# Layer-1 FFN of a vision tower: the elementwise work of GpSimd moves to VectorE, with a new order of the pieces

## The chip, the cores and the metric

The kernel runs on one core of a Trainium2 chip. A core has five engines with a queue each, which run on their own and wait for each other by semaphores: PE (TensorE, matmuls into PSUM), DVE (VectorE), ACT (ScalarE), POOL (GpSimd) and SP (SyncE, which here issues nearly all DMA transfers). An engine takes its queue in order, so an instruction that waits holds up all that stand behind it. The metric is the device time of one execution in microseconds (us), taken as the median of several runs.

## The reference, cut to what matters

32 images of 256 tokens with 256 features pass through a tokenizer and two layers, each with an attention and an FFN block, all in float32. The change lies in the FFN of layer 1. With four heads of 64 features and four experts a head it computes, for each image:

```python
sx = jnp.einsum('bsh,ndh->bnsd', x, hl_w) + hl_b[None, :, None, :]
q, k, v = ...                                    # from sx; q for each of 4 experts
att = jax.nn.softmax(scores + causal, axis=-1)
qkv = jnp.einsum('bnest,bntd->bnesd', att, v)
gs = jax.nn.softmax(einsum(out, gate_w) + gate_b, axis=-1)
mixed = jnp.einsum('bnsed,bnse->bnsd', out.reshape(b, nh, s, ne, d), gs)
hn = layernorm(mixed + resid, ln_g, ln_b)
hx = relu(fx @ fc1_w.T + fc1_b) @ fc2_w.T + fc2_b   # fx is hn, head by head
hx = layernorm(hx + fx, fnorm_g, fnorm_b)
fg = jax.nn.softmax(fout @ fgate_w.T, axis=-1)      # fout is hx, heads joined
h = h + fout.reshape(b, s, nh, d) * fg[..., None]
```

In `setup_inputs` the gain `fnorm_g` is all ones and the bias `fnorm_b` all zeros.

## The kernel before

The activations of all images stay in SBUF, in 32 tiles `H[b]` of 128 partitions by 512 elements (two blocks `c` of 128 tokens, 256 features each). The stages before, up to about 1229 us, are the tokenizer, layer 0 and the attention of layer 1. The change leaves them alone.

The FFN of layer 1 is cut into pieces, listed in `PIECES` by number. A piece is a small function that issues a few instructions of one engine for one image `b`: `heads` (PE), `heads_out` (ACT copies and two transfers on SP), `experts`, `head_values`, six parts of `scores` (PE), their `exponentials` (ACT) and `later_keys` (POOL, a select that zeroes the keys after the query), eight `outputs` (PE) and `outputs_out` (ACT copies to `eo`), the softmax of the experts' gate (`gate_logits`, `gate_softmax`, DVE with one exponential on ACT), `mixed` and `summed` (the experts' weighted sum), a norm (`squares` on ACT, `squares_sum` on DVE, `root` on ACT, `scaled`), `turn_e`, `moved_e` and `turned_e` (a transpose of 32x32 blocks, written to DRAM and read back turned), the two small layers `first_layer` and `second_layer` with `features_moved` for their input, and at the end the heads' gate (`head_gate`) and the final norm (`last_norm`), which writes the image out.

The order in which the pieces are issued is written by hand as numbers. `ROUND` is a list of pairs (offset, piece): one pass over it issues each piece once, each for the image that lies the offset ahead, so that about eight images are in work at once. Round after round is issued until the last image has had its `heads`; the list `END` issues what is then left. A manual schedule keeps each engine's queue in this order, and semaphores are put in where data or buffers require it. So in a steady round PE, DVE, ACT, POOL and SP do exactly one image's worth of work each.

Buffers matter too. There are eight PSUM banks, handed out in turn by `bank()`: the ninth request waits until the first has been emptied. Tiles from the pool `e_1` have one buffer for each name. The tile called `esq` holds in turn the first norm's squares, the result of the block transpose (`turn_e`, L1359), and the second norm's squares.

The places that are touched: `mixed` (L1316) multiplies the experts' outputs `eo` by their gate in two halves of 1024 elements, the first on DVE, the second on POOL. `summed` (L1326) adds the halves. `head_gate` 9 (L1458) multiplies the norm's factor `fv` by the heads' gate. `last_norm` (L1460 to L1481) computes `ey * fv` and times the gain `fn_g` on DVE, bias times gate (`fadd`, L1470) and plus `H[b]` (L1474) on POOL, adds both on DVE (L1477) and stores the sum.

Of the kernel before, what the change touches and what calls it, by code (L numbers as in the profile page):

```python
# [35 lines left out]
ALU = mybir.AluOpType  # L36
# [5 lines left out]
B, N, D = 32, 256, 256  # L42
# [38 lines left out]
def vit_tower(tc, a, out):  # L81
# [38 lines left out]
    def over(ap, shape, axis):  # L120
        return ap.unsqueeze(axis).to_broadcast(shape)
# [987 lines left out]
    with (  # L1109
# [205 lines left out]

        def mixed(b, im, k):  # L1316
            x = experts_of(im, k, MIX, HD)
            (nc.vector if k == 0 else nc.gpsimd).tensor_tensor(  # L1318
                x, x, over(im.gate[:, :, 2 * k : 2 * k + 2], [P, NG, 2, HD], 3), ALU.mult
            )  # L1320

# [33 lines left out]
        def turn_e(b, im):  # L1355
            if b == B - 1:
                im.pt = feature_major(im.whole["er"].rearrange("p (c n) d -> p c (n d)", c=NC))
                return
            y = whole(im, "esq", G8, key="blocks").rearrange("p g d -> p (g d)")  # L1359
            nc.vector.transpose(  # L1360
                y.rearrange("p (f s t) -> p s f t", f=4, t=32),
                im.whole["er"].rearrange("p (c k m) d -> p k c (m d)", c=2, k=2),
            )
            im.d = dram.tile([2, 4, 32, N], F32, name="er_turned", bufs=4)
            nc.sync.dma_start(im.d.rearrange("m i q x -> (i q) m x"), y.rearrange("p (m x) -> p m x", m=2))
# [65 lines left out]
        def head_gate(b, im, i):  # L1431
# [22 lines left out]
                nc.vector.reciprocal(im.m, im.m)  # L1454
            if i == 8:
                nc.vector.tensor_tensor(im.gate, im.gate, over(im.m, [P, NC, NH], 2), ALU.mult)
            if i == 9:
                nc.vector.tensor_tensor(im.rs, im.rs, im.gate.rearrange("p c n -> p (c n)"), ALU.mult)  # L1458

        def last_norm(b, im, i):  # L1460
            if i == 0:
                f = whole(im, "fout", G8)
                nc.vector.tensor_tensor(f, im.whole["ey"][:, :, 0:HD], over(im.rs, G8, 2), ALU.mult)  # L1463
            if i == 1:
                f = im.whole["fout"]
                nc.vector.tensor_tensor(f, f, over(row_e("fn_g"), G8, 1), ALU.mult)  # L1466
            if i == 2:
                w = whole(im, "fadd", G8)
                nc.gpsimd.tensor_tensor(
                    w, over(row_e("fn_b"), G8, 1), over(im.gate.rearrange("p c n -> p (c n)"), G8, 2), ALU.mult  # L1470
                )
            if i == 3:
                w = im.whole["fadd"]
                nc.gpsimd.tensor_tensor(w, w, H[b].rearrange("p c (n d) -> p (c n) d", d=HD), ALU.add)  # L1474
            if i == 4:
                f = im.whole["fout"]
                nc.vector.tensor_tensor(f, f, im.whole["fadd"], ALU.add)  # L1477
                nc.sync.dma_start(
                    out[b].rearrange("(c p) d -> p c d", p=P),
                    f.rearrange("p (c n) d -> p c (n d)", n=NH),  # L1480
                )  # L1481

        images = [Image() for _ in range(B)]
        PIECES = (
            (features_in,), (residual,), (moved_e,), (heads,), (heads_out,), (experts, 0), (experts_out, 0),
# [10 lines left out]
            (squares_sum, 0), (root, 0), (scaled,), (turn_e,), (turned_e,), (features_zero,), (first_layer,),  # L1496
            (first_layer_out,), (second_layer,), (second_layer_out, 0), (second_layer_out, 1), (squares, 1),
            (squares_sum, 1), (root, 1), (head_gate, 0), (head_gate, 1), (head_gate, 2), (head_gate, 3),
            (head_gate, 4), (head_gate, 5), (head_gate, 6), (head_gate, 7), (head_gate, 8), (head_gate, 9),
            (last_norm, 0), (last_norm, 1), (last_norm, 2), (last_norm, 3), (last_norm, 4),  # L1500
            (features_moved,),
        )
        ROUND = (
            (-11, 9), (-12, 6), (-10, 54), (-7, 85), (-10, 55), (-7, 86), (-10, 56), (-7, 87), (-10, 57),
            (-11, 30), (-13, 3), (-10, 58), (-11, 10), (-8, 69), (-11, 17), (-7, 89), (-8, 70), (-13, 4),
            (-13, 1), (-11, 25), (-11, 23), (-12, 12), (-11, 11), (-12, 16), (-7, 88), (-12, 22), (-10, 59),
            (-7, 90), (-11, 29), (-8, 68), (-13, 7), (-9, 2), (-12, 18), (-11, 36), (-10, 60), (-11, 27),
            (-10, 61), (-11, 33), (-11, 44), (-8, 71), (-11, 32), (-10, 62), (-13, 8), (-11, 31), (-11, 40),
            (-8, 72), (-11, 41), (-10, 63), (-8, 73), (-7, 91), (-8, 74), (-10, 64), (-12, 24), (-8, 75),
            (-11, 39), (-11, 34), (-8, 76), (-11, 38), (-11, 35), (-8, 77), (-11, 42), (-8, 78), (-11, 43),  # L1510
            (-11, 37), (-12, 14), (-11, 46), (-11, 45), (-10, 65), (-11, 47), (-8, 79), (-12, 28), (-12, 15),
            (-11, 48), (-8, 80), (-8, 81), (-11, 49), (-9, 67), (-12, 20), (-11, 50), (-12, 26), (-13, 5),
            (-8, 82), (-12, 13), (-11, 51), (-9, 92), (-11, 52), (-10, 66), (-8, 83), (-15, 0), (-11, 53),
            (-12, 21), (-8, 84), (-12, 19),
        )
        END = (
            (2, 10), (3, 58), (4, 2), (2, 25), (2, 27), (2, 11), (5, 69), (3, 59), (6, 88), (5, 70), (2, 17),
            (1, 16), (1, 9), (3, 60), (0, 4), (1, 10), (2, 31), (3, 61), (2, 23), (5, 68), (2, 36), (2, 39),
            (2, 33), (1, 22), (3, 62), (3, 63), (4, 67), (5, 71), (2, 35), (2, 29), (2, 38), (5, 72),
            (5, 73), (1, 11), (4, 92), (2, 34), (3, 64), (3, 65), (2, 37), (5, 74), (5, 75), (6, 89),  # L1520
            (2, 44), (2, 41), (1, 28), (2, 32), (2, 42), (6, 90), (1, 17), (2, 43), (3, 66), (5, 76), (0, 2),
            (6, 91), (2, 46), (2, 40), (5, 77), (5, 78), (5, 79), (2, 45), (2, 47), (2, 48), (5, 80),
            (1, 23), (2, 49), (1, 29), (0, 7), (5, 81), (2, 50), (1, 14), (2, 51), (2, 52), (2, 53), (5, 82),
            (4, 69), (2, 54), (2, 55), (0, 5), (0, 8), (1, 15), (5, 83), (4, 70), (1, 20), (2, 56), (1, 13),
            (5, 84), (2, 57), (2, 58), (0, 6), (0, 12), (1, 12), (1, 21), (1, 19), (0, 16), (0, 18), (1, 18),
            (3, 2), (4, 71), (4, 68), (2, 59), (1, 38), (1, 27), (2, 60), (4, 72), (2, 61), (1, 25), (1, 36),
            (1, 37), (4, 73), (1, 24), (0, 22), (1, 32), (2, 62), (1, 26), (1, 35), (0, 24), (3, 67),
            (5, 85), (2, 63), (5, 89), (1, 46), (4, 74), (1, 45), (2, 64), (5, 86), (1, 44), (5, 90),
            (1, 33), (5, 87), (4, 75), (4, 76), (3, 92), (5, 88), (2, 65), (2, 66), (1, 31), (1, 39),
            (1, 34), (1, 40), (1, 43), (1, 41), (1, 42), (1, 47), (1, 48), (1, 49), (0, 14), (4, 77),  # L1530
            (1, 50), (4, 78), (1, 51), (4, 79), (0, 20), (3, 69), (1, 52), (1, 53), (3, 70), (1, 54),
            (0, 15), (1, 55), (0, 13), (0, 9), (0, 26), (0, 17), (0, 21), (4, 80), (1, 56), (1, 57), (4, 81),
            (0, 10), (2, 2), (3, 68), (0, 11), (4, 82), (1, 58), (4, 83), (0, 23), (4, 84), (0, 31), (4, 85),
            (0, 19), (1, 59), (3, 71), (0, 25), (0, 27), (3, 72), (1, 60), (0, 30), (0, 33), (2, 67),
            (1, 61), (0, 32), (3, 73), (0, 34), (0, 28), (0, 39), (1, 62), (0, 35), (0, 43), (0, 29),
            (2, 68), (0, 36), (1, 63), (0, 40), (5, 91), (0, 42), (1, 64), (3, 74), (2, 92), (1, 65),
            (0, 44), (4, 89), (0, 37), (0, 38), (3, 75), (4, 86), (0, 41), (0, 46), (0, 45), (1, 66),
            (0, 47), (3, 76), (0, 48), (3, 77), (0, 49), (3, 78), (0, 50), (2, 69), (3, 79), (2, 70),
            (0, 51), (0, 52), (4, 87), (0, 53), (0, 54), (0, 55), (1, 2), (2, 71), (3, 80), (4, 90), (0, 56),
            (3, 81), (0, 57), (3, 82), (0, 58), (1, 67), (4, 88), (1, 69), (1, 92), (2, 72), (3, 83),  # L1540
            (0, 59), (3, 84), (0, 60), (3, 85), (0, 61), (4, 91), (0, 62), (2, 73), (1, 70), (0, 63),
            (2, 74), (0, 64), (1, 68), (2, 75), (2, 76), (0, 65), (2, 77), (3, 86), (2, 78), (2, 79),
            (3, 89), (3, 87), (2, 80), (0, 66), (2, 81), (1, 71), (2, 82), (3, 90), (0, 67), (3, 88),
            (2, 83), (1, 72), (2, 84), (3, 91), (2, 85), (1, 73), (0, 92), (1, 74), (1, 75), (1, 30),
            (1, 76), (1, 77), (2, 89), (2, 86), (0, 69), (1, 78), (2, 87), (1, 79), (1, 80), (2, 90),
            (1, 81), (2, 88), (0, 70), (1, 82), (1, 83), (0, 71), (1, 84), (2, 91), (1, 85), (0, 72),
            (1, 89), (0, 73), (1, 86), (0, 74), (0, 75), (1, 87), (0, 76), (0, 77), (0, 78), (0, 79),
            (1, 90), (0, 80), (0, 81), (1, 88), (0, 82), (0, 83), (0, 84), (1, 91), (0, 85), (0, 89),
            (0, 68), (0, 86), (0, 87), (0, 90), (0, 88), (0, 91),
        )  # L1550
        LATE = {1: B // 2 - 2, 2: B // 2 - 1}
        LAST = PIECES.index((heads,))

        def order_e():
# [422 lines left out]
```

## Time and profile before

| what | value |
|---|---|
| median of 3 runs | 1882.4 us (1880.36 to 1883.76) |
| the profiled execution's own time | 1881.05 us |
| its span, first to last instruction | 1879.3 us |
| mean granted TensorE clock | 0.99 |
| start of the layer-1 FFN (first load of `exT`) | 1228.9 us |
| distance of rounds from 1343 us to 1790 us | 18.62 us |
| last `heads`, where `END` begins | 1790.5 us |

The profile shows one execution. Busy times of an engine are the union of its instructions; the ends of matmuls are modelled, so PE seems busier than it is. In a windows row the columns are the stretch, its length, then for PE, PEld (weight loads), DVE, ACT and POOL the busy time with the number of instructions, then the granted clock, the DMA share and GB/s. In a timeline row they are start, duration, engine, line, operation, output<-inputs, the shapes and the number of instructions merged. In a waits row: who waited, for whom, total us, times, longest. A wait for several semaphores is put down to the one that came last.

### The profile page before, as it was taken

The numbers are of one execution on the slowest core, as the hardware profiler recorded it, in microseconds if no ns is written. First come the engines' busy times: TensorE is split into PE (matmuls) and PEld (weight loads), VectorE is DVE, ScalarE is ACT, GpSimd is POOL, SyncE is SP. The second block draws the span as 40 slices with busy tenths as digits, with TensorE's granted clock in tenths as the row PEclk, the third lists the DMA queues.
The fourth block names the chain that finished last, engine by engine and source line by source line (L and its number), as shares of the span: only waits on it lengthen the run. The fifth ranks groups of instructions, "written<-read, shape, count | busy, mean of one in ns | idle before, by whom it ended". The sixth has DMA issues, their size and how long they took to land. (4 is left out here: it accounts for less than half of the span.)

```text
span 1879.3 us, 36625 instructions
## 1 busy us (share of the span) xinstructions
PE 1829.4 (97%) x14282; PEld 1286.5 (68%) x14282; DVE 1346.5 (72%) x3336; ACT 800.0 (43%) x1640; POOL 827.1 (44%) x792
## 2 busy tenths in 40 slices
PE   9999999999999999999999999999999999999993
PEld 7887567676767676766655555567877777787872
DVE  2335376878787674534578778746899989998998
ACT  0001222222222212121344554557878787877772
POOL 1224133434343334243353433424575757676653
PEclk9999999999999999999999999999999999999995
DMA  8540221212121134233222222122343333333332
GB/s 302 162 153 19 46 56 45 68 45 64 38 63 39 68 120 138 85 118 93 87 79 79 79 79 79 68 79 61 92 106 98 103 103 98 103 98 103 97 86 69
DMA packets 193171, 167.50 MB, mean 89 GB/s; under 512 B 70880, under 2 KB 166112, under 8 KB 192608
## 3 DMA queue, kind: packets, MB, share of 16 engines
q1 hardware_dynamic: 186272, 147.51, 27.3%
q0 software_dynamic: 6144, 16.79, 2.9%
q8 instruction: 115, 1.88, 0.4%
q10 hardware_dynamic: 576, 0.79, 0.1%
q14 instruction: 64, 0.52, 0.1%
HBM read 82.98 MB, written 57.41 MB: 75 GB/s over the span
## 5 line engine op out<-in xcount | busy, mean ns | idle before, releaser
L1237 POOL TENSOR_SCALAR_AFFINE_SELECT et<-et 128x1024 f32<-128x1024 f32 (+1 forms) x192 | 199.4, 1059 | 206.5 <-ACT et L1228 185.7
L118 PE MATMUL bank<-ev,et 128*64 128x72 f32 (+1 forms) x6144 | 204.2, 225 | 3.9 <-DVE ev L1203 2.3
L118 PEld LDWEIGHTS bank<-ev,et 128*64 128x64 f32 x6144 | 193.3, 137 | 17.7 <-POOL fadd L1474 7.6
L1228 ACT ACTIVATE et<-bank 128x512 f32<-128x512 f32 x384 | 199.6, 624 | 3.1 <-PE bank L118 1.7
L118 PE MATMUL bank<-g,sx 64*128 64x512 f32 (+1 forms) x512 | 194.4, 501 | 0.3 <-ACT g L1190 0.3
L118 PE MATMUL bank<-g,sw 64*128 64x512 f32 (+1 forms) x512 | 189.9, 501 | 0.9 <-DVE ev L1203 0.9
L118 PE MATMUL bank<-tokW,patch 128*128 128x256 f32 x768 | 166.6, 379 | 3.1 <-DMA patch<-in_patches_dram 3.1
L118 PEld LDWEIGHTS bank<-tokW,patch 128*128 128x128 f32 x768 | 145.9, 190 | 24.1 <-issue 3.9
L118 PE MATMUL bank<-bxT,w_wuv 128*128 128x512 f32 x300 | 131.4, 592 | 2.5 <-DMA bxT<-b_turned 2.5
L864 ACT ACTIVATE hT<-bank,cols 128x512 f32<-128x512 f32 x64 | 43.6, 687 | 187.3 <-PE bank L118 120.2
L118 PE MATMUL bank<-wvo,dm 128*128 128x512 f32 x256 | 114.3, 599 | 0.0
L118 PE MATMUL bank<-w_wo,gT 128*128 128x256 f32 x512 | 113.2, 379 | 0.0
L118 PE MATMUL bank<-attn,bv 128*128 128x256 f32 x512 | 113.1, 379 | 0.0
L118 PE MATMUL bank<-w_w,hT 128*128 128x256 f32 x512 | 112.3, 379 | 0.0
L118 PE MATMUL bank<-xsel,w_w 128*128 128x512 f32 x256 | 111.4, 592 | 0.0
L118 PEld LDWEIGHTS bank<-attn,bv 128*128 128x128 f32 x512 | 97.2, 190 | 19.6 <-issue 7.2
L118 PEld LDWEIGHTS bank<-g,sx 64*128 64x128 f32 x512 | 88.1, 186 | 31.4 <-issue 21.8
L126 DVE BATCH_NORM_STATS2 six<-h 128x6 f32<-128x256 f32 x256 | 105.6, 412 | 4.4
L118 PEld LDWEIGHTS bank<-w_w,hT 128*128 128x128 f32 x512 | 97.0, 190 | 15.6 <-issue 2.9
L118 PEld LDWEIGHTS bank<-w_wo,gT 128*128 128x128 f32 x512 | 97.2, 190 | 13.4 <-DVE gT L489 0.2
L151 POOL TENSOR_SCALAR rs_c<-st_c 128x4 f32<-128x4 f32 x16 | 3.0, 190 | 234.4 <-DVE st_c L127 234.4
L118 PE MATMUL bank<-w_wuv,bxT 128*128 128x512 f32 x240 | 105.4, 592 | 0.0
(289 smaller groups left out, 3814.6 us busy)
## 6 DMA issues: line engine op xcount, KB each, us to landing
patch<-in_patches_dram SPq DMA_DIRECT2D x31, 768.0 KB
exT<-normed SPq DMA_DIRECT2D x32, 256.0 KB
sw<-sx SPq DMA_DIRECT2D x64, 128.0 KB
out_dram<-fout SPq DMA_DIRECT2D x32, 256.0 KB
er_turned<-esq SPq DMA_DIRECT2D x31, 256.0 KB
fraw<-er_turned SPq DMA_DIRECT2D x62, 128.0 KB
both<-fxT SPq DMA_DIRECT2D x62, 128.0 KB
both<-hx SPq DMA_DIRECT2D x62, 128.0 KB
```

Source lines behind the costliest of these rows:

```text
L118: nc.tensor.matmul(o, lhsT, rhs, start=first, stop=last)
L126: nc.vector.bn_stats(six, x)
L151: nc.gpsimd.tensor_scalar(o, var, 1.0, 1e-5, ALU.mult, ALU.add)
L864: nc.scalar.activation(s.hT[:, m, :], p, AF.Gelu_apprx_tanh, bias=col("b1", m))
L1228: nc.scalar.activation(t2[:, i, :], p, AF.Exp)
L1237: nc.gpsimd.affine_select(out=own, in_=own, pattern=[[0, 2 * n_e], [1, P]], compare_op=ALU.is_ge, fill=0.0, base=0, channel_multiplier=-1,)
```

## The change

- `mixed` runs both halves on DVE.
- `last_norm` runs wholly on DVE. It is now: `ey * fv` (part 0), times `fn_g` (part 1), plus `fn_b` (part 2), and then for each of the eight groups of 64 features (two token blocks, four heads) one `scalar_tensor_tensor`, which multiplies by the heads' gate, a scalar for each token, and adds `H[b]` (parts 3 and 4). Part 5 is the store. `head_gate` 9 and the tile `fadd` are gone. In the new lists part 2 stands ahead of part 1.
- POOL is left with the six selects of `later_keys` in each round.
- The block transpose of `turn_e` writes to a tile of its own, `eblk`.
- `ROUND` and `END` are new. On PE a round now begins with `experts` 0 and three parts of `scores`, has `experts` 1, `head_values`, `first_layer`, `heads` and the other three parts of `scores` next, and ends with `second_layer` and the eight `outputs`. On DVE the two halves of the mix stand next to each other with `scaled` between, `turn_e` comes after them and ahead of the second norm's squares, and the eight operations of the final norm follow the last product of `head_gate`. `LATE` is only moved in the text.

```diff
         def mixed(b, im, k):
             x = experts_of(im, k, MIX, HD)
-            (nc.vector if k == 0 else nc.gpsimd).tensor_tensor(
+            nc.vector.tensor_tensor(
                 x, x, over(im.gate[:, :, 2 * k : 2 * k + 2], [P, NG, 2, HD], 3), ALU.mult
             )
...
-            y = whole(im, "esq", G8, key="blocks").rearrange("p g d -> p (g d)")
+            y = whole(im, "eblk", G8).rearrange("p g d -> p (g d)")
...
-            if i == 9:
-                nc.vector.tensor_tensor(im.rs, im.rs, im.gate.rearrange("p c n -> p (c n)"), ALU.mult)
 
         def last_norm(b, im, i):
+            f = whole(im, "fout", G8)
             if i == 0:
-                f = whole(im, "fout", G8)
                 nc.vector.tensor_tensor(f, im.whole["ey"][:, :, 0:HD], over(im.rs, G8, 2), ALU.mult)
             if i == 1:
-                f = im.whole["fout"]
                 nc.vector.tensor_tensor(f, f, over(row_e("fn_g"), G8, 1), ALU.mult)
             if i == 2:
-                w = whole(im, "fadd", G8)
-                nc.gpsimd.tensor_tensor(
-                    w, over(row_e("fn_b"), G8, 1), over(im.gate.rearrange("p c n -> p (c n)"), G8, 2), ALU.mult
-                )
-            if i == 3:
-                w = im.whole["fadd"]
-                nc.gpsimd.tensor_tensor(w, w, H[b].rearrange("p c (n d) -> p (c n) d", d=HD), ALU.add)
-            if i == 4:
-                f = im.whole["fout"]
-                nc.vector.tensor_tensor(f, f, im.whole["fadd"], ALU.add)
+                nc.vector.tensor_tensor(f, f, over(row_e("fn_b"), G8, 1), ALU.add)
+            if i in (3, 4):
+                for n in range(NH):
+                    g, d = (i - 3) * NH + n, slice(n * HD, (n + 1) * HD)
+                    nc.vector.scalar_tensor_tensor(
+                        f[:, g, :], f[:, g, :], im.gate[:, i - 3, n : n + 1], H[b][:, i - 3, d], ALU.mult, ALU.add
+                    )
+            if i == 5:
                 nc.sync.dma_start(
...
         PIECES = (
...
-            (head_gate, 4), (head_gate, 5), (head_gate, 6), (head_gate, 7), (head_gate, 8), (head_gate, 9),
-            (last_norm, 0), (last_norm, 1), (last_norm, 2), (last_norm, 3), (last_norm, 4),
+            (head_gate, 4), (head_gate, 5), (head_gate, 6), (head_gate, 7), (head_gate, 8), (last_norm, 4),
+            (last_norm, 0), (last_norm, 1), (last_norm, 2), (last_norm, 3), (last_norm, 5),
...
         ROUND = (
-            (-11, 9), (-12, 6), (-10, 54), (-7, 85), (-10, 55), (-7, 86), (-10, 56), (-7, 87), (-10, 57),
...
+            (-1, 84), (-4, 43), (-5, 27), (-4, 46), (-6, 5), (-5, 13), (-4, 44), (-6, 6), (-1, 85), (-1, 86),
+            (-1, 90), (-5, 19), (-5, 25), (-5, 12), (-5, 28), (-2, 2), (-2, 67), (-4, 47), (-4, 48),
...
+            (-5, 40), (-5, 38), (-2, 80), (-5, 35), (-2, 81), (-2, 88), (-2, 82), (-5, 36), (-2, 83),
```

## The prediction

> **What bounds the kernel now.** I read the page's busy table first, then the span by windows, then the waits of a steady stretch, and last the timelines of single rounds.
>
> ```profile
> PE 1829.4 (97%) x14282; PEld 1286.5 (68%) x14282; DVE 1346.5 (72%) x3336; ACT 800.0 (43%) x1640; POOL 827.1 (44%) x792
> ```
>
> PE at 97% looks like the answer, but the ends of matmuls are modelled. The windows view (length, then busy time of PE, PEld, DVE, ACT, POOL) of four rounds of the layer-1 FFN says more. The cuts are where PE starts the `heads` matmuls of one image and of the next.
>
> ```profile
> 1307.50:1325.40 17.90, 17.90 (x301) 14.21 (x299) 12.46 (x38) 15.10 (x37) 7.49 (x8) 1.00 0.36 91
> 1325.40:1343.30 17.90, 17.90 (x301) 14.38 (x299) 16.20 (x38) 14.21 (x36) 11.78 (x9) 1.00 0.36 90
> 1343.30:1361.90 18.60, 18.58 (x300) 14.73 (x298) 16.90 (x40) 14.57 (x37) 12.33 (x9) 1.00 0.38 100
> 1641.50:1660.10 18.60, 18.58 (x300) 14.76 (x298) 16.90 (x41) 14.57 (x37) 12.32 (x9) 1.00 0.39 100
> ```
>
> PE does the same work in all four. While the pipeline of images fills, DVE has 12.46 us of work and the round takes 17.9. From the third on DVE has 16.90 and the round takes 18.62, unchanged until 1790 us. So 17.87 (starts 1307.5, 1325.4, 1343.3) is what PE needs, and the 0.75 above it comes from the loop through DVE. The waits of PE over 18 steady rounds (total, times, longest) agree:
>
> ```profile
> PEld bank L118 <- DVE ev L1203: 12.0, 18, 0.7
> PEld bank L118 <- ACT g L1190: 2.9, 17, 0.2
> ```
>
> One pair of score matmuls in each round waits for the PSUM bank that DVE empties at L1203; in the round at 1641 its second half starts 0.40 late (1646.15, 1646.55). A second wait of about 0.2 stands behind ACT's copy of `g`.
>
> Why DVE is slow is in the timelines of DVE and POOL (start, duration; in brackets the idle time before and who ended it):
>
> ```profile
> 1306.87 1.22 DVE L1318 TENSOR_TENSOR eo<-eo,gate 128x1024 f32<-128x1024 f32 x1
> 1642.15 2.94 DVE L1318 TENSOR_TENSOR eo<-eo,gate 128x1024 f32<-128x1024 f32 x1
> 1647.04 2.29 DVE L1326 TENSOR_TENSOR two<-eo 128x1024 f32<-128x1024 f32 x1
> 1649.86 0.97 DVE L1329 TENSOR_TENSOR er<-two 128x512 f32<-128x512 f32 x1
> ```
>
> ```profile
> 1641.72 2.29 POOL L1318 TENSOR_TENSOR eo<-eo,gate 128x1024 f32<-128x1024 f32 x1 [0.43 <-DVE gate L1314]
> 1643.97 2.02 POOL L1469 TENSOR_TENSOR fadd<-rows_e,fgate 128x512 f32<-128x512 f32 x1
> 1646.55 1.70 POOL L1474 TENSOR_TENSOR fadd<-fadd,h 128x512 f32<-128x512 f32 x1
> 1648.21 4.74 POOL L1237 TENSOR_SCALAR_AFFINE_SELECT et<-et 128x1024 f32<-128x1024 f32 x4
> ```
>
> The two engines take turns. POOL's half of the mix ends at 1644.01, and DVE's, begun at 1642.15, ends 1.08 later. POOL's `fadd` ends at 1648.25, and `two` ends 1.08 later. Begun ahead of POOL (1306.87), DVE's mix takes 1.22. So a DVE operation with two SBUF inputs that meets a running POOL operation waits for its end, then runs at its own speed.
>
> [...] The zero counts at L1172, with one tensor input, take 0.67 beside POOL work too. [...]
>
> **The change part by part, per round.** Costs on DVE are start-to-start distances in the round at 1641.
>
> - Half of the mix moves from POOL to DVE: one more 1024-element product, 1.22 long, 1.13 to its successor. POOL's 2.29 goes, and DVE's own half no longer waits: 2.86 becomes 1.13. Net on DVE 1.13 - 1.73 = -0.60.
> - The two `fadd` operations leave POOL (2.02 + 1.70). `two` no longer waits behind the second: 2.22 becomes 1.13, -1.09.
> - The final norm: the last addition (L1477, 0.60 apart) and the small product L1458 (0.11) go; an addition of the bias comes, as L1466, 0.63. Eight `scalar_tensor_tensor` of 64 elements come. No row has that form. [...] Below: independent 48-element products L1287 start 0.11 apart, 0.9 for eight. They don't wait for each other, so I take 0.13 each, 1.05. Net +0.97.
> - Sum: 16.90 - 0.60 - 1.09 + 0.97 = 16.2 busy on DVE. Of this about 0.7 is the wait of L1329 and L1332 behind selects (0.97 and 1.00 against 0.68), which the new order may keep or move.
> - POOL keeps six selects: 12.3 - 2.29 - 2.02 - 1.70 = 6.3, less for those that now don't wait (0.63 and 1.09 free, against means of 0.86 and 1.59).
> - DVE behind selects: bounded by none, and by all of them standing in front of a two-input operation, 4 x 0.5 + 2 x 1.0 = 4. Laying the new order beside PE's pieces, selects 4, 0, 5 and 3 fall under `junk`, the transpose, PSUM evictions or a reduction, and selects 1 and 2 hold up one operation each. I take 1.0 in all, i.e. 0.3 above the old 0.7: 16.5.
> - Waits of DVE for ACT: 14.3 + 9.1 over 18 rounds, 1.3 a round. The one for `fv` (0.6) stays, since `root` and the first gate product still follow each other; those for `esq` (0.8) get covers: zero counts and a small reduction before the first, `summed` before the second. So DVE needs 16.5 + 0.6 = 17.1, under PE's 17.87.
> - The own buffer of the turned result: `esq` held both squares and the transposed block. The new order puts the transpose before the second squares, so in one buffer these would wait for the store. With its own buffer this costs nothing; SBUF stays level, `fadd` being gone.
> - The order on PE: the same pieces with the same four changes of tile shape[...], in one round. So 17.87 holds for it. What could be late: `scores` 4 needs `experts_out` 1, which ACT reaches after some 7.2 us of its own work (0.96 + 0.95 + 0.76 + 0.95 + 0.54 + 0.95 + 0.2 + 0.6 + 0.96, plus hops), from about 1.2 us into the round; PE gets there at 9.15, so some 0.7 is spare. `second_layer` needs the two transfers of `hx`: issued 0.5 apart, landing about 2.0 after issue (packets after 1645.1), ready near 9.9 with PE there at 11.0.
> - The SP queue keeps eleven transfers a round. The store of `out` now waits for the last of the eight operations, with the moves of `fxT` and `hx` behind it. They follow by over 1 us in the plan, so nothing queues.
> - The six images of the ending: before, DVE is full from 1830 to 1850 (19.92 of 20). There the mix adds 1.2 for three images, the norm 1.0 for six, and waits behind POOL of about 9 us go (rows such as 2.3 and 2.4 for single 0.68 operations). I count it at nothing. In the last image the store is issued at 1874.5, 5.4 after the last gate (1869.05), because the range flag's operations stand between. After, the eight operations come first, 1.2, and the flag's 3.3 follow: about 2 us gained.
>
> **Sum.** I take a round of 18.0, leaving 0.13 for hops. 25 rounds stand at 18.62: 25 x 0.62 = 15.5. With the ending 17.5. The profiled execution took 1881.05 (span 1879.3), so 1863.5; the median of the runs is 1.35 higher: 1865.
>
> **Rivals.**
> - *Only part is gained*: selects or ACT cost DVE 1 to 2 us more, and the round is 18.2 to 18.5: 25 x 0.12 to 0.42 plus 2, so 1870 to 1877. For: ACT waits recur in the old order. Chance 0.15.
> - *DVE is still the bound*: the selects in front of two-input operations cost about 2.5, so 16.2 - 0.7 + 2.5 + 0.6 = 18.6: 1879 to 1886, no difference. For it: both L1329 and L1332 wait today. Against: only 6 us of POOL remain. Chance 0.10.
> - *Slower*: ACT takes its queue in order, and the softmax exponential of the experts' gate stands ahead of `first_layer_out` and `experts_out` 1. When DVE comes to the gate's subtraction more than about 0.7 later than laid out, ACT stands, then `scores` 4, `scores` 3 and all of PE behind. It decides once the loop through both passes 18.7. At 19.0 a round: 25 x 0.4 = 10 more, 1892. For it: DVE carries six dependent gate steps with no slack of their own, and ran late in the old order. Against: 0.7 spare on ACT, more DVE time free. Chance 0.20.
>
> **How the numbers follow.** The likeliest case (0.55) is a round of 17.87 to 18.15, 1860 to 1869, at 1865. With the partial gain, faster is 0.70, same 0.10, slower 0.20; 0.2% (3.8 us) is about what a measurement tells from no change. The range runs from 1857 (the floor with 5 us of the ending) to 1888, leaving out about a tenth on either side.
>
> **What would show it.** Right: mix products near 1.2 on DVE twice a round, `two` near 1.2, DVE busy 16 to 17 a round, starts of `heads` 17.9 to 18.1 apart, and no regular wait of PE for DVE. Wrong: PE waiting for `g` or for a bank behind ACT in each round (slower), or DVE two-input rows still over 1 us with rounds of 18.6 (no gain)[...].

## The result, and the profile after

| | before | after |
|---|---|---|
| median of four runs each, us | 1883.08 (1880.36 to 1884.35) | 1864.3 (1862.13 to 1866.7) |
| ratio after/before, 95% interval | | 0.990 (0.988 to 0.992) |
| profiled execution's own time; span, us | 1881.05; 1879.3 | 1866.7; 1864.9 |
| mean distance of the last 24 starts of `heads`, us | 18.63 | 17.87 |
| from the last `heads` to the end of the span, us | 88.8 | 86.9 |

The forecast was 1865.0 with a range of 1857 to 1888. The busy table of the page after:

```profile
PE 1815.6 (97%) x14282; PEld 1274.4 (68%) x14282; DVE 1349.6 (72%) x3592; ACT 811.0 (43%) x1640; POOL 615.6 (33%) x696
```

Shares of the whole span tell almost nothing of what happened. DVE has as much to do as before (1349.6 against 1346.5), and PE is at 97% in both. Only POOL has visibly less, by 211 us. The windows of single rounds, cut at the starts of `heads` as for the kernel before (length, then PE, PEld, DVE, ACT, POOL, then clock, DMA share, GB/s):

```profile
1330.84:1349.20 18.36, 18.12 (x300) 14.32 (x299) 16.53 (x48) 15.02 (x38) 5.07 (x6) 1.00 0.39 102
...
1640.00:1657.86 17.86, 17.86 (x306) 14.21 (x302) 16.73 (x48) 15.04 (x37) 5.32 (x6) 1.00 0.42 106
```

Most rounds now take 17.86, the length that PE alone had needed while the pipeline of images was filling before the change; the last of the filling, at 1330.84, takes 18.36. DVE's 16.73 is 0.17 less than the old 16.90, so a smaller busy time of DVE is not what freed 0.76 a round. What changed is who waits for whom. First a row of the waits of the kernel before that the prediction makes no use of, over 22 steady rounds (total us, times, longest):

```profile
ACT esq L1337 <- DVE er L1332: 44.3, 22, 2.1
```

ScalarE stood 2.0 us in every round before the first norm's squares, with its later work behind it, because DVE had not finished `er`. That wait lies on the chain of work that ended last. The chain is followed back from the last instruction, at each step to what released it. Between 1400 and 1760 us it runs through DVE for 74% and through ScalarE for 22% of the time, and never through PE. In the round at 1642 it has these steps (start, length):

```profile
1650.86 1.02 DVE er L1332
1651.88 0.02 issue
1651.90 0.63 ACT esq L1337
```

In the changed kernel the same chain between 1400 and 1760 us is PE's matmuls alone:

```profile
by line: PE bank L118 100.1%
```

The waits after, over 23 rounds:

```profile
...
ACT sx L1162 <- PE bank L118: 16.9, 23, 0.7
...
ACT g L1190 <- PE bank L118: 12.5, 23, 0.6
DVE lg L1434 <- ACT fv L1349: 12.2, 20, 0.6
...
PEld bank L118 <- ACT g L1190: 5.4, 23, 0.2
```

The wait for `er` is no longer among them, nor is PE's for L1203. ScalarE now waits for PE instead, 0.7 a round for `sx` and 0.5 for `g`. Of PE's regular waits for another engine, 0.2 for `g` is left. DVE's wait for `fv` stays, 0.6 a round. The timeline of DVE in the round at 1640 (start, duration):

```profile
1641.31 1.22 DVE L1326 TENSOR_TENSOR two<-eo 128x1024 f32<-128x1024 f32 x1
...
1646.87 1.66 DVE L1469 SCALAR_TENSOR_TENSOR fout<-fout,fgate,h 128x64 f32<-128x64 f32 x8
...
1648.97 0.69 DVE L1329 TENSOR_TENSOR er<-two 128x512 f32<-128x512 f32 x1
...
1649.73 0.68 DVE L1332 TENSOR_TENSOR er<-er,res 128x512 f32<-128x512 f32 x1
...
1654.53 1.23 DVE L1318 TENSOR_TENSOR eo<-eo,gate 128x1024 f32<-128x1024 f32 x1
...
1656.27 1.22 DVE L1318 TENSOR_TENSOR eo<-eo,gate 128x1024 f32<-128x1024 f32 x1
```

Both products of the mix and `two` run at their own speed (1.22), where the old rows said 2.94 and 2.29. The additions to `er` no longer wait behind selects.

Where the time went, from the profiles of before and of a second execution of the same changed kernel (`changed_again`, below): the first `heads` starts 0.6 later (1240.1 against 1239.5), the eight starts that fill the pipeline take 2.9 longer (106.67 against 103.72), the next 24 rounds take 17.9 less (429.3 against 447.2), the ending 1.7 less (87.17 against 88.83). Together that is -16.1, the difference of the two spans. The medians of all runs lie 18.8 apart; the profiles show one execution each.

### The profile page after: what moved, and what is told of

It reads as the page before. It is cut to its first block, busy times and chain, and to the rows that moved or that the text cites. A ratio compares the mean times of both kernels' runs of the same rounds, so it can differ in the third digit from the quotient of the medians.

```text
span 1864.9 us, 36574 instructions
## 1 busy us (share of the span) xinstructions
PE 1815.6 (97%) x14282; PEld 1274.4 (68%) x14282; DVE 1349.6 (72%) x3592; ACT 811.0 (43%) x1640; POOL 615.6 (33%) x696
## 4 chain that ended last, share of the span: by engine, by line
PE 91%; DVE 6%; ACT 1%; DMA 1%; issue 1%; SPq 0%; ACTq 0%; DVEq 0%
PE bank L118 90%; DVE fout L1469 1%; DVE eo L1318 0%; DMA patch<-in_patches_dram 0%; PE bank L516 0%; DVE two L1326 0%; DVE ranges L1341 0%; DVE six L126 0%; DVE junk L1172 0%; DVE ey L1426 0%; ACT dex L945 0%; DVE dz L991 0%; DVE fout L1465 0%; DVE fout L1461 0%; DVE dxB L199 0%
## 5 line engine op out<-in xcount | busy, mean ns | idle before, releaser
L1237 POOL TENSOR_SCALAR_AFFINE_SELECT et<-et 128x512 f32<-128x512 f32 (+1 forms) x192 | 169.3, 891 | 397.0 <-ACT et L1228 282.2
L118 PE MATMUL bank<-ev,et 128*64 128x68 f32 (+1 forms) x6144 | 193.4, 224 | 0.8 <-POOL et L1237 0.6
L118 PE MATMUL bank<-g,sw 64*128 64x256 f32 (+1 forms) x512 | 180.3, 490 | 0.0
L118 PE MATMUL bank<-g,sx 64*128 64x256 f32 (+1 forms) x512 | 179.3, 490 | 0.3 <-ACT g L1190 0.3
L118 PEld LDWEIGHTS bank<-g,sx 64*128 64x128 f32 x512 | 92.2, 187 | 54.3 <-issue 45.0
L118 PEld LDWEIGHTS bank<-bxT,w_wuv 128*128 128x128 f32 x300 | 58.0, 194 | 69.9 <-issue 68.9
```

Source lines behind the costliest of these rows:

```text
L118: nc.tensor.matmul(o, lhsT, rhs, start=first, stop=last)
L1237: nc.gpsimd.affine_select(out=own, in_=own, pattern=[[0, 2 * n_e], [1, P]], compare_op=ALU.is_ge, fill=0.0, base=0, channel_multiplier=-1,)
```

## The experiments

The theory after the result: the round is at PE's floor because two things came together. No operation of DVE stands behind a two-input one of POOL any more, and the new order has DVE deliver what ScalarE and PE wait for in time. The rivals: the engines alone did it, whatever the order; or the order alone did it, whatever the engines. A third question was how far DVE is from being the bound again.

| run | median, us | ratio to before, 95% interval | mean of the last 24 rounds, us | ending, us |
|---|---|---|---|---|
| old_order: new operations, old order | 1939.2 | 1.030 (1.028 to 1.031) | 20.57 | 97.9 |
| old_order_later: the same, eight operations later | 1905.0 | 1.011 (1.010 to 1.013) | 19.20 | 98.3 |
| mix_alone_old: mix on DVE, all else old | 1906.7 | 1.012 (1.010 to 1.014) | 19.65 | 87.8 |
| order_new: old operations, new order | 1947.5 | 1.034 (1.032 to 1.035) | 20.66 | 100.9 |
| half_mix_pool: changed, half of the mix back | 1885.5 | 1.002 (1.001 to 1.002) | 18.50 | 92.0 |
| pool_adds_unread: changed, POOL work added | 1901.9 | 1.010 (1.008 to 1.012) | 18.95 | 98.7 |
| two_counts_unread: changed, DVE work added | 1898.8 | 1.009 (1.008 to 1.011) | 18.88 | 97.7 |
| esq_shared: changed, one buffer again | 1890.3 | 1.003 (1.002 to 1.004) | 18.87 | 88.3 |
| changed_again: as it is | 1864.1 | 0.990 (0.988 to 0.991) | 17.89 | 87.2 |
| two_products | 1860.3 | 0.988 (0.986 to 0.990) | 17.91 | 83.2 |
| two_products2 | 1860.5 | 0.988 (0.986 to 0.990) | 17.89 | 82.6 |
| ending_scalar | 1869.6 | 0.993 (0.991 to 0.994) | 17.90 | 90.6 |

"Ending" is from the last `heads` to the end of the span; rounds and endings are from the profiles.

### The new operations in the old order

`old_order` is the kernel before with the new engines. The old lists call the parts of the norm in their own sequence, so these are counted as they come:

```diff
-            (nc.vector if k == 0 else nc.gpsimd).tensor_tensor(
+            nc.vector.tensor_tensor(
...
         def last_norm(b, im, i):
+            f = whole(im, "fout", G8)
+            i = im.part = getattr(im, "part", -1) + 1
...
+            if i == 3:
+                for g in range(NG):
+                    c, n = g // NH, g % NH
+                    nc.vector.scalar_tensor_tensor(
+                        f[:, g, :], f[:, g, :], im.gate[:, c, n : n + 1], H[b][:, c, n * HD : (n + 1) * HD],
+                        ALU.mult, ALU.add,
+                    )
```

> The operations of the changed kernel (both halves of the mix and the whole final norm on VectorE, selects alone on GpSimd) in the old order of the pieces; the squares and the turned block share a buffer as in the kernel before. Theory (VectorE's loop sets the old round, and it is made of busy time plus waits for ScalarE that only the new order covers): 16.90 - 0.60 - 1.09 + 1.49 (eight operations at the measured 0.196 apart) = 16.7 busy, 0.2 less than before, with the waits for ScalarE of 1.3 a round left where they are: a round of 18.3 to 18.5, 1873 to 1880 us. Rival (the engines alone do it, the order is of no account): rounds of 17.9, 1863 to 1867. Second rival (the gain is the order's alone): 18.6 or more, 1881 and above.

It took 1939.2 us, 57 more than before, with rounds of 20.57. The theory missed, and the rival that said the engines alone suffice missed most. The second rival's bound (1881 us and above) holds, but it named no loss of this size, and the run with the new order and the old operations, below, speaks against it. From the waits of 22 rounds:

```profile
ACT esq L1337 <- DVE er L1332: 58.2, 14, 4.2
...
PE bank L118 <- ACT g L1190: 41.5, 22, 1.9
```

ScalarE stands 4.2 us a round (the other eight of its 22 waits are put down to the store of `out`, but end with `er` too, as below), `g` is copied late, and PE waits for it. This run still shares one buffer between the squares and the turned block, but no wait of ScalarE for the store of the block is on the list. The timelines of DVE, POOL and ACT show why:

```profile
1642.14 3.66 DVE L1470 SCALAR_TENSOR_TENSOR fout<-fout,fgate,h 128x64 f32<-128x64 f32 x8
...
1646.32 0.68 DVE L1329 TENSOR_TENSOR er<-two 128x512 f32<-128x512 f32 x1
1647.04 0.69 DVE L1332 TENSOR_TENSOR er<-er,res 128x512 f32<-128x512 f32 x1
...
1641.30 3.63 POOL L1237 TENSOR_SCALAR_AFFINE_SELECT et<-et 128x1024 f32<-128x1024 f32 x4 [3.46 <-ACT et L1228]
...
1647.76 0.63 ACT L1337 ACTIVATE esq<-er 128x512 f32<-128x512 f32 x1 [4.16 <-DMA out_dram<-fout]
```

The eight small operations stand ahead of the two additions to `er`, and take 3.66 instead of 1.66. One by one, the first started at 1642.14 and the next ones at 1643.17, 1643.76, 1644.35 and 1644.93, while selects of POOL started at 1643.13, 1643.72 and 1644.31: one operation of each engine in turn, 0.59 apart, and from then on 0.196. Each of the first four had to let a select finish. ScalarE starts its squares 0.03 us after `er` is done.

So the same operations are 75 us slower in the other order. How much of that is the place of the eight alone? They were moved behind `summed` 2 in `ROUND`, and nothing else:

```diff
-            (-7, 90), (-11, 29), (-8, 68), (-13, 7), (-9, 2), (-12, 18), (-11, 36), (-10, 60), (-11, 27),
-            (-10, 61), (-11, 33), ...
+            (-11, 29), (-8, 68), (-13, 7), (-9, 2), (-12, 18), (-11, 36), (-10, 60), (-11, 27),
+            (-10, 61), (-7, 90), (-11, 33), ...
```

> The new operations in the old order, as in the run old_order, with one move: the eight small operations of the final norm are issued after the last addition of the experts' sum (L1332 of the kernel before) instead of ahead of its first. Theory (in old_order ScalarE stood 4.2 us a round before the first norm's squares, because the eight, four of them held up by selects, were ahead of the sum that it needs): this wait goes, VectorE has 16.7 to 17.0 of work and 1.3 to 1.8 of waits, rounds of 18.2 to 18.8, 1872 to 1890 us, so the place of eight operations was worth some 2 us a round. Rival (the old order as a whole does not suit the new operations): rounds above 19.5, 1910 and more.

1905.0 us, rounds of 19.20: 1.37 less a round. ScalarE's wait for `er` fell from 4.2 to 1.3, as expected, but a wait for the other norm's input, `ey`, of 1.5 a round stood in its place. The bounds of theory and rival lie on either side of this result. The place of the eight operations is worth 34 of the 57 us lost; what in the old order costs the rest was not taken apart.

### One edit alone in the kernel before

`mix_alone_old` changes a single line of the kernel before (the first two lines of the diff above).

> One edit of the change alone, in the kernel before: both halves of the mix on VectorE, with the old order and the old final norm (bias times gate and the addition of H[b] on GpSimd). Theory (VectorE's own half stops waiting for GpSimd's, as the prediction's first step has it: -0.60 on VectorE, up to half of it lost again to GpSimd's product, which now starts 2.3 us earlier and meets the mix): rounds of 18.0 to 18.4, 1867 to 1877 us. Rival (the old order does not suit an operation on another engine, as in the two runs with the whole new work in it): 18.7 and more, 1884 us and above.

1906.7 us, rounds of 19.65: the rival held. The prediction's step that this edit takes 0.60 off DVE is wrong in this surrounding. From the timelines of DVE and POOL:

```profile
1641.32 1.53 DVE L1463 TENSOR_TENSOR fout<-ey,fv 128x512 f32<-128x512 f32 x1
1642.78 1.65 DVE L1318 TENSOR_TENSOR eo<-eo,gate 128x1024 f32<-128x1024 f32 x1
...
1644.95 1.69 DVE L1318 TENSOR_TENSOR eo<-eo,gate 128x1024 f32<-128x1024 f32 x1
...
1641.22 1.08 POOL L1469 TENSOR_TENSOR fadd<-rows_e,fgate 128x512 f32<-128x512 f32 x1 [0.17 <-DVE gate L1312]
1642.27 1.09 POOL L1237 TENSOR_SCALAR_AFFINE_SELECT et<-et 128x512 f32<-128x512 f32 x1
1643.32 2.24 POOL L1474 TENSOR_TENSOR fadd<-fadd,h 128x512 f32<-128x512 f32 x1
```

With its half of the mix gone, POOL comes to `fadd` 2.5 us earlier, as seen from the gate, and meets DVE's product with `fv` (1.53 instead of 0.68). The first half of the mix then waits for a select and the second for POOL's addition (1.65 and 1.69 instead of 1.22). The second half shows the turns once more: POOL's addition ends at 1645.56, DVE's product, begun at 1644.95, ends 1.08 later. The count of zeros between them, with one input, takes its 0.67 beside POOL's addition. DVE is busy for 17.95 us in most rounds instead of 16.9, about as much more as the round is longer. In the kernel before, `fadd` had lain in part under the count and the reads of PSUM (1645.01 to 1646.50 there, 0.67 for the count and 0.48 for each read); started earlier, it meets more of DVE's two-input operations.

### The new order with the old operations

`order_new` is the changed kernel with POOL's old work: half of the mix, `fadd` as bias times gate plus `H[b]`, and on DVE one product with the gate and one addition of `fadd`.

```diff
-            nc.vector.tensor_tensor(
+            (nc.vector if k == 0 else nc.gpsimd).tensor_tensor(
...
-            if i == 2:
-                nc.vector.tensor_tensor(f, f, over(row_e("fn_b"), G8, 1), ALU.add)
...
+            if i in (3, 4) and "fadd" not in im.whole:
+                w = whole(im, "fadd", G8)
+                nc.gpsimd.tensor_tensor(
+                    w, over(row_e("fn_b"), G8, 1), over(im.gate.rearrange("p c n -> p (c n)"), G8, 2), ALU.mult
+                )
+                nc.gpsimd.tensor_tensor(w, w, H[b].rearrange("p c (n d) -> p (c n) d", d=HD), ALU.add)
+                nc.vector.tensor_tensor(
+                    f, f, over(im.gate.rearrange("p c n -> p (c n)"), G8, 2), ALU.mult
+                )
+            elif i in (3, 4):
+                nc.vector.tensor_tensor(f, f, im.whole["fadd"], ALU.add)
```

> The new order with GpSimd's old work: half of the mix, bias times gate and the addition of H[b] run on GpSimd, VectorE then multiplies by the gate and adds GpSimd's result. Theory (taking turns; the parts measured one by one cost 0.49 and 1.00 a round): both together 18.9 to 19.9, with VectorE waiting for the sum besides, 1893 to 1925 us; so neither the order alone nor the engines alone give the gain. Rival (the gain is the order's): below 1875.

1947.5 us and 20.66 a round, worse than the range of the theory and far from the rival. DVE had only 15.71 busy in the round at 1702: as little work as in any run, and the slowest rounds of all. From the waits of 22 rounds:

```profile
POOL fadd L1466 <- DVE fgate L1456: 112.5, 22, 5.7
...
DVE fout L1474 <- POOL fadd L1469: 50.3, 22, 2.3
...
DVE two L1326 <- POOL eo L1318: 25.6, 16, 1.6
```

DVE waits 2.3 us a round for POOL's sum, which the new order never meant it to wait for, and POOL itself stands 5.1 for the gate. This is how the run is built: the pair on POOL is issued just ahead of the DVE operations that use it, where the kernel before had some 5 us between. Another place for the pair in the new order was not tried. With this all four combinations are measured: old operations in the old order 1883, new in the old 1939, old in the new 1948, new in the new 1864. As built here, each half of the change alone is a loss of 3%; together they gain 1%.

### What each piece of POOL work costs in the new order

`half_mix_pool` puts one line back:

```diff
-            nc.vector.tensor_tensor(
+            (nc.vector if k == 0 else nc.gpsimd).tensor_tensor(
                 x, x, over(im.gate[:, :, 2 * k : 2 * k + 2], [P, NG, 2, HD], 3), ALU.mult
```

> The changed kernel with one part undone: the second half of the mix runs on GpSimd again; order and all else stay. Theory [...]: VectorE is rid of 1.13 us, but its own half or the scaling beside it waits for GpSimd's 2.29, so its work grows by 1.2 a round, more than its slack of about 0.5: rounds of 18.4 to 18.7, 1878 to 1886 us. Rival (an operation moved to the other engine runs beside it, VectorE has less to do): 1862 to 1867.

1885.5 us, rounds of 18.50. The size is right and the mechanism is not: DVE's own half took 1.23, it did not wait. POOL reached its half late, at 1651.35, because a select, 1.09 long from 1650.30, stood ahead of it in its queue, and DVE then stood for the result:

```profile
DVE two L1326 <- POOL eo L1318: 35.2, 22, 1.7
```

That is 1.6 us a round of waiting for data, not for a turn.

`pool_adds_unread` adds POOL work on which no data depend, issued at the last product of the heads' gate:

```diff
+            if i == 4:
+                w = p1.tile(G8, F32, name="unread")
+                nc.gpsimd.tensor_tensor(w, over(row_e("fn_b"), G8, 1), over(row_e("fn_g"), G8, 1), ALU.mult)
+                nc.gpsimd.tensor_tensor(w, w, H[b].rearrange("p c (n d) -> p (c n) d", d=HD), ALU.add)
```

> The changed kernel with two additional GpSimd operations a round (a product and a sum of 512 elements from SBUF into a tile that nobody reads), issued where the last product of the heads' gate stands. No data depend on them, VectorE's own instructions are unchanged. Theory (taking turns): they cost VectorE between one and both of their free times of about 1.0 each, against a slack of about 0.5: rounds of 18.4 to 19.4, 1878 to 1903 us. Rival (the two engines only share bandwidth, and what moved to VectorE mattered by its data dependences): within 4 us of 1864.

1901.9 us, rounds of 18.95 on average and 18.86 in most. The theory held. DVE and POOL in the round at 1650:

```profile
1657.76 1.58 DVE L1326 TENSOR_TENSOR two<-eo 128x1024 f32<-128x1024 f32 x1
...
1660.66 1.78 DVE L1461 TENSOR_TENSOR fout<-ey,fv 128x512 f32<-128x512 f32 x1
...
1658.24 2.25 POOL L1474 TENSOR_TENSOR unread<-rows_e 128x512 f32<-128x512 f32 x1
1660.57 1.33 POOL L1475 TENSOR_TENSOR unread<-unread,h 128x512 f32<-128x512 f32 x1
```

The product with `fv` starts at 1660.66, stands until POOL's sum ends at 1661.90, and is done at 1662.44: 1.78 instead of 0.68. The turns go both ways: POOL's product, begun behind `two`, takes 2.25, where the shortest of the run's 32 takes 1.27. DVE's busy time rose by 1.26 to 17.99, the round by 1.00. No engine waits for POOL in this run's list of waits, so late selects are not the cause. That taking turns alone, with no data in play, costs a microsecond a round is shown by this run.

### How near DVE is to the bound

`two_counts_unread` adds DVE work after the eight, of a form that took no turn in `mix_alone_old` (a count of 512 elements, 0.67 beside POOL's addition):

```diff
+            if i == 3:
+                w, n = p1.tile([P, 2 * N], F32, name="unread"), p1.tile([P, 2], F32, name="unread_n")
+                for k in range(2):
+                    nc.vector.tensor_scalar(
+                        w, f.rearrange("p g d -> p (g d)"), 0.0, 0.0, ALU.is_equal, ALU.add, accum_out=n[:, k : k + 1]
+                    )
```

> The changed kernel with two additional VectorE operations a round after the eight of the final norm (counts of zeros over 512 elements, one SBUF input, result unread), 1.21 us in all. VectorE has 16.73 busy and, going by the run with unread GpSimd additions (17.99 busy in a round of 18.86), 0.87 of waits that stay. Theory (slack of VectorE 0.3): 16.73 + 1.21 + 0.87 = 18.8 a round, and 6 x 1.2 in the ending: 1890 to 1897 us. Rival (VectorE has the 0.76 of slack that the prediction laid out): rounds of 18.3, 1880 us.

Most rounds took 18.79, 0.93 more than 17.86 for 1.21 of work: a slack of 0.28, the work that DVE can take on before the round grows. The run before (1.26 busy, 1.00 longer: 0.26) gives the same answer, with the work added at another place. The time, 1898.8, is 2 above the range because the ending grew by 10.5 (97.7 against 87.2) and not by 7.

### The buffer of its own

```diff
-            y = whole(im, "eblk", G8).rearrange("p g d -> p (g d)")
+            y = whole(im, "esq", G8, key="blocks").rearrange("p g d -> p (g d)")
```

> The changed kernel with the turned block in the buffer of the squares again, one edit undone. Theory (in the new order the second squares follow the transpose, so ScalarE would wait for the store, 2.7 us from issue to landing): squares about 1.2 us later, ScalarE's copies and exponentials behind them, the norm's factor later by as much; with about 0.5 of slack a round of 18.3 to 18.9 and 1875 to 1893 us. Rival (the store has long landed, the buffer is of no account): 1864.

1890.3 us, rounds of 18.87, and 23 waits of a kind that the changed kernel has not:

```profile
ACT esq L1337 <- DMA er_turned<-esq: 57.0, 23, 3.7
```

ScalarE stands 2.5 us a round for the store of the turned block. Without the one line about a buffer, the new order would have been slower than the kernel before.

### Eight small operations or two large ones

```diff
-            if i in (3, 4):
-                for n in range(NH):
-                    g, d = (i - 3) * NH + n, slice(n * HD, (n + 1) * HD)
-                    nc.vector.scalar_tensor_tensor(
-                        f[:, g, :], f[:, g, :], im.gate[:, i - 3, n : n + 1], H[b][:, i - 3, d], ALU.mult, ALU.add
-                    )
+            if i == 4:
+                nc.vector.tensor_tensor(
+                    f, f, over(im.gate.rearrange("p c n -> p (c n)"), G8, 2), ALU.mult
+                )
+            if i == 3:
+                nc.vector.tensor_tensor(f, f, H[b].rearrange("p c (n d) -> p (c n) d", d=HD), ALU.add)
```

> The changed kernel with the eight operations of 64 elements replaced by one product with the gate spread over 64 elements and one addition of H[b], of 512 elements each: 2 x 0.60 instead of 1.57, 0.37 less on VectorE a round. Theory (TensorE sets the round at 17.86): the same within 0.2%, 1861 to 1867 us, rounds of 17.86. Rival (VectorE still sets it): 9 us less, 1855.

In this form four of the six images of the ending are computed otherwise, since `END` issues part 3 ahead of part 4 there: `H[b]` is added before the product with the gate. The operations and their number are the same. It took 1860.3 us with rounds of 17.86, so the rounds are PE's as the theory has it, but 4 us went all the same, from the ending. `two_products2` has the product first for every image (the first of the two calls multiplies, the second adds), beside an unchanged kernel:

> The changed kernel with the eight operations of 64 elements replaced by one product with the gate and one addition of H[b] of 512 elements each, in this order for every image. Theory (the rounds are TensorE's, but VectorE is full for 70 us of the ending, where six images' final norms still come): rounds of 17.86 as in the changed kernel, and 6 x 0.37 = 2.2 us off the ending, more where selects held single ones of the eight up: 1860 to 1862 us, a ratio to the changed kernel in the same set of 0.998 to 0.999. Rival (no difference; the 1860.3 of the run with the two in the other order for some images was the set's): the same median within 1.5 us.

> The changed kernel as it is, beside the variant with two products, on the same chip. Expected 1864 us, and, if the 3.3 us that its first profiled execution lost at about 200 us (in a stage that no edit touches) belong to that execution alone, a profile whose first heads start at 1239.7 to 1240.5 instead of 1242.9. If they belong to the program, 1242.9 again.

1860.5 us (1858.94 to 1861.36) against 1864.1 (1862.34 to 1865.59), in the same set: 3.6 us less, and no run of one among those of the other. The two profiled executions lie 6.0 apart, and 4.6 of that is the ending, 82.6 against 87.2; the rounds are the same. The windows of the whole ending and of its third 20 us, first of the unchanged kernel:

```profile
1776.10:1863.30 87.20, 53.84 (x897) 39.99 (x895) 78.29 (x229) 45.50 (x113) 14.39 (x14) 0.77 0.28 75
1816.10:1836.10 20.00, 6.76 (x79) 3.92 (x74) 19.90 (x61) 7.95 (x21) 0.00 (x0) 0.68 0.37 97
```

and of the kernel with two products:

```profile
1774.62:1857.20 82.58, 52.01 (x897) 39.25 (x895) 73.92 (x190) 45.64 (x112) 16.98 (x14) 0.79 0.29 79
1814.60:1834.60 20.00, 7.75 (x70) 4.83 (x69) 19.70 (x56) 6.78 (x18) 0.00 (x0) 0.60 0.36 94
```

In the third 20 us DVE is full while PE has 7 of 20. Over the whole ending DVE has 78.3 to do in the one and 73.9 in the other, 4.4 less for an ending 4.6 shorter. From its start to the next operation the pair takes 1.33 where nothing holds it up, and the eight take 1.57: 1.4 in six images, not the 2.2 that was expected. Single ones of the eight again stand behind a select, for 1.9 in all (four in the ending take 0.65 to 1.11 instead of 0.28), and one addition of the pair for 0.4. The remaining 1.5 stays open. This variant beats both kernels.

The second execution of the unchanged kernel also settled an oddity: its first `heads` start at 1240.1. In the first profile of the changed kernel it was 1242.9, of which 3.2 us appeared at about 200 us, where the program is that of before. They belong to that execution.

### DVE's work in the ending given to ScalarE

```diff
             r = im.whole["er"]
+            if b >= B - 3:
+                for g in range(NG):
+                    nc.scalar.mul(r[:, g, :], r[:, g, :], im.rs[:, g : g + 1])
+                return
...
+            if i == 0 and b >= B - 4:
+                for g in range(NG):
+                    nc.scalar.mul(f[:, g, :], im.whole["ey"][:, g, 0:HD], im.rs[:, g : g + 1])
```

> The variant with two products, and in the ending alone the scaling of the first norm (last three images) and of the second (last four) as eight ScalarE multiplications by a per-token scalar each, instead of one VectorE operation: 7 x 0.60 = 4.2 us less on VectorE, 56 small operations more on ScalarE. Theory (VectorE is full from 1778 to 1858 and sets the ending, ScalarE is free for more than half of it): rounds unchanged, 1 to 4 us off the ending, 1856.5 to 1859.5 us. Rival (ScalarE's eight small operations are in the chain of dependences in place of one): 1860 to 1863.

1869.6 us, and an ending of 90.6 instead of 82.6: the rival held, and more than it said. Over the whole ending DVE had 70.7 us to do instead of 73.9, 3.2 less, and the ending was 8 us longer. ScalarE's timeline in the last image, and a row of its waits:

```profile
1855.43 2.02 ACT L1466 ACTIVATE fout<-ey,fv 128x64 f32<-128x64 f32 x8 [1.12 <-DMA out_dram<-fout]
1857.35 0.19 ACT L1453 ACTIVATE fgate<-fgate 128x8 f32<-128x8 f32 x1
```

```profile
DVE eblk L1364 <- ACT er L1355: 5.9, 2, 3.9
```

The eight take 2.0 in place of 0.6, first wait 1.1 for the store of the image before, and the gate's exponential, which DVE's next steps need, queues behind them. What it is worth to take work off a full engine depends on where the work goes: 4.4 less on DVE took 4.6 off the ending in `two_products2`, and 3.2 less put 8.0 on it here, where the work joined ScalarE's queue.

## Why the prediction was right, and where it was not

- **The bound.** Right: 17.87 was taken from PE's starts while the pipeline filled, and the rounds are now 17.86. The changed order of PE's pieces left it so, and the chain that ended last runs through PE alone.
- **The mix, -0.60, and `two`, -1.09.** Right in the changed kernel (1.23, 1.22 and 1.22 long). Not a property of the edit: alone in the old order it made the same products 1.65 and 1.69 (`mix_alone_old`). In the old order the step does not hold with the rest of POOL's work in place. One reading was off too: the 2.29 that the prediction has for POOL's half of the mix is not POOL's own speed, it holds a wait for the DVE product begun before it. Without a wait the same operation takes 1.92 (`half_mix_pool`), 1.6 times DVE's 1.22.
- **The eight operations, 1.05 at 0.13 apart.** Wrong in size. They are 0.28 long and 0.196 apart, 1.57 in all. The 0.13 was my estimate from the 48-element products at L1287, which start 0.11 apart; their pace is not that of the eight. DVE's spare time covered the difference, 0.52 a round. With 1.57 the sum of the ledger is 16.7 instead of 16.2.
- **Selects, 0.3 more than before.** They cost no more than before: they now hold up L1303 (0.62, not 0.19) and L1312 (0.37, not 0.18) instead of L1329 and L1332. Busy time came to 16.73 against the predicted 16.5.
- **Waits for ScalarE, 0.6, and so 0.76 of slack.** The wait for `fv` is as predicted. The slack is 0.28 by two runs. The ledger was 0.23 short in busy time, and 0.3 a round of waits that stay (0.87 in place of 0.6) was not in it.
- **The round of 18.0.** The 0.13 laid aside for hops was not needed. The prediction counted 25 rounds at 18.62, but from 1343 to 1790 us there are 24, so its own sum is 24 x 0.62 = 14.9; they gave 17.9.
- **The buffer of its own, nothing.** Right as it is. The step gave no price for leaving it out; that is 1.0 a round.
- **The queue of SP, and the slack of `scores` 4 and `second_layer`.** No regular wait of PE shows there in the changed kernel. I did not test how much is spare.
- **The ending, -2.** -1.9 in the profiled execution and -1.7 in the other. That DVE's work there is neutral was only the sum of two halves; the run with two products shows that the eight alone are worth some 4 us of it.
- **What the sum left out.** The filling of the pipeline, eight starts, takes 2.9 longer. With 2.4 more gained in the rounds than the 15.5 of the prediction, the two errors nearly cancel. That the total came out within a microsecond is in part luck.
- **The rivals.** The slower one named ScalarE's queue, held up by DVE, with `scores` and PE behind it. That is what happens in `old_order` (4.2 us of ScalarE a round, 41.5 us of PE in 22 rounds), at another instruction than I named, the squares and not the exponential. The prediction had looked at DVE's waits for ScalarE and at PE's; the row of ScalarE's wait for DVE (2.0 a round in the kernel before) would have shown what the order had to mend.

## What to carry to other kernels

Where two engines take turns, as DVE and POOL do here, an order of instructions is made for one division of the work: it lays the long operations of one engine beside operations of the other that take no turn, as the count does here (0.67 beside POOL's addition). Moving an operation without a new order, or taking a new order without moving it, can lose more than both together gain, as in the four combinations here (1939 and 1948 us for one without the other, 1883 for neither, 1864 for both); try them together, and judge neither by its half. And before a queue is thought safe, read the waits of every engine for every other, not only those of the busiest.

## What the runs showed of the hardware

- DVE's two-input operations and POOL's operations alternated one at a time: four selects and four of the eight small operations went in turn, 0.59 apart (`old_order`), so each of these four, 0.196 apart where POOL is idle, waited for a select. The eight lost 2.0 to a busy POOL there; the one large `two` lost 0.4 to a select in `pool_adds_unread`.
- Both sides wait: POOL's product of 512 elements took 1.27 at its shortest and 2.25 behind `two` (`pool_adds_unread`), its addition 1.26 at its shortest in the kernel before and 2.24 in `mix_alone_old`.
- An eight-part `scalar_tensor_tensor` over 64 elements each (1.57, `changed_again`) cost more than a product and an addition of 512 (1.33, `two_products2`), though it reads and writes less in all.
- ScalarE's multiplication of 64 elements by a per-token scalar came every 0.24 us, eight of them 2.0, against 0.60 for the one DVE operation that they replace (`ending_scalar`).
